# Cross attention of layer 0: spreading the inverse row sums to the channels through DRAM instead of by TensorE transposes

## The chip, the cores and the metric

The kernel runs on one core of a Trainium2 chip. A core has five engines with an instruction stream each: TensorE (PE, matmuls and transposes into PSUM), VectorE (DVE), ScalarE (ACT), GpSimd (POOL) and SyncE (SP, which here only issues DMAs). Each engine works its stream strictly in order and waits on semaphores of the others. Sixteen DMA engines move data between DRAM and the on-chip memory SBUF. The metric is the device time of one execution in microseconds (us), as a median of several runs.

## What is computed

A decoder of two layers on 32 sequences of 128 tokens of 128 channels. Layer 0 is a recurrent mixing block (rwkv), a cross attention over a context, and a mixture of experts; layer 1 is a causal attention, a windowed cross attention and a quantised projection. The change lies in layer 0's cross attention, with 16 heads of 64 channels, whose keys and values are extended by 128 learned memory rows, and in the copies of the rwkv block ahead of it:

```python
q = (queries @ wq_w + wq_b).reshape(B, S, H, DK).transpose(0, 2, 1, 3)
k_ext = jnp.concatenate([keys @ wk_w + wk_b, broadcast(mk)], axis=1)
v_ext = jnp.concatenate([values @ wv_w + wv_b, broadcast(mv)], axis=1)
...
scores = jnp.einsum('bhsd,bhtd->bhst', q, k) / jnp.sqrt(jnp.float32(DK))
attn = jax.nn.softmax(scores, axis=-1)
out = jnp.einsum('bhst,bhtd->bhsd', attn, v)
return out.transpose(0, 2, 1, 3).reshape(B, S, H * DV) @ wo_w + wo_b

# rwkv, per head, for every step t:
state = state * jnp.exp(w_t)[..., None] + k_t[..., None] * v_t[..., None, :]
o_t = jnp.einsum('bhkv,bhv->bhk', state, r_t)
```

## The kernel before

The 32 sequences ("blocks") are worked in ten groups of 2, 2, 2, 4, 4, 4, 4, 4, 4 and 2 blocks. For each group g the kernel records three pieces of work for layer 0: `rwkv(g)`, `xattn0(g)` and `route(g)` (the choice of experts and the scatter of tokens to DRAM). After the ninth group come 22 blocks of expert work, then the rest of the experts and layer 1.

*What sets the order.* Nothing is issued where it is written. The helpers `V`, `A`, `G`, `M` and `S` record an operation for DVE, ACT, POOL, PE or SP with an expected duration, its reads and writes, for a DMA the time to landing, and a wished time `plan.at` (in units of four blocks). `Plan.run` then plays these through against a list of engines, buffers and PSUM banks: at each moment an engine takes the ready operation with the earliest wished time. The table `SHIFTS` adds a correction to the wished time of each kind of operation ("DVE sc# nm#" is the row maximum), one table for each layer. The result is one fixed order on each engine; the expected times only serve to make it. Waits at run time are semaphores that follow from the real tiles. So a change of an operation or of a shift can move every instruction of layer 0.

*`xattn0(g)`.* For each of eight channel chunks c (two heads, 128 channels) PE projects keys, queries and values (L764, L767, L774). Then, for two blocks at a time, `slot` computes scores (L843), DVE takes the negative row maximum (L848), ACT the exponentials with their row sums `xsm` as a by-product (L855), PE transposes the exponentials (L865), and DVE and ACT copy these out of PSUM (L871, L869). `attend` (L796) makes `av`: channels on the partitions, tokens along the free dimension, not yet divided by the row sums.

The row sums stand the other way round, one value for each token (partition), block and head. The division takes these steps: DVE forms the reciprocals `xrs` (L803); POOL widens each to 64 columns (`wide`, L805); PE transposes that, one 128x128 transpose for each block, into the PSUM bank `over` (L810); ACT copies it to SBUF (`overs`, L814); DVE multiplies `av` by it into `xoT` (L816). After eight chunks PE projects `xoT` to the output (L823).

*`rwkv(g)`.* The recurrence runs as eight scans on DVE (L684), one for each j of a head's eight value channels; scan j needs channel j of each head of v and r copied to all eight rows of that head. For groups with `early` set, PE does this with a selecting matmul for each j (L640), and PE also sums the eight products r in PSUM (L694, eight matmuls). For the other groups SP stores v and r to DRAM (`spill_v`, `spill_r`, L646) and loads each j as a broadcast (L650), and POOL adds up the eight products (L690), so that L694 has one matmul. `early` is `g < 3`.

*SP's queue.* All plain DMAs are issued by SP in one order: first loads, then `clear` (L891), which writes 17 MB of zeros to the table `xreg`, then the spills and broadcasts, context loads, and after layer 0's attention the experts' weights (L1107) and token rows (L1114). The weights need the block table, which DVE writes (L1071).

Of the kernel before, what the change touches and what calls it, by code (L numbers as in the profile page):

```python
# [48 lines left out]
for _name, _n in (("wo_b", D), ("bo", D), ("b_proj", D), ("f_b", D), ("d_act", 1)):  # L49
# [22 lines left out]


SHIFTS = [{
    "ACT cen#ps# cen#": 0.09, "ACT cen#ps# sq#": -0.22, "ACT g#ps# gate#": -1.15, "ACT h#ps# wb#": 0.6,
    "ACT k#ps# k#sb#": 1.44, "ACT moe#xnT#p moe#xnT#": -0.38, "ACT over# overs#": 0.06,
    "ACT r#ps# r#sb#": 0.94, "ACT rw#xnp# xp#": -0.02, "ACT sc# nm#": 0.91, "ACT th#": -0.06,
    "ACT tr# eT#": 0.72, "ACT v#ps# v#sb#": 0.7, "ACT w#ps# dec#": -0.97, "ACT xa#xnT#p xa#xnT#": 0.04,
    "ACT xk#ps# xk#": -0.61, "ACT xq#ps# xq#": 0.67, "ACT xv#ps# xv#": 0.59, "DVE": 0.2,
    "DVE av# overs#": -0.05, "DVE bv#ps": 0.83, "DVE bv#row": -1.07, "DVE dec# v#": 1.2, "DVE fw#src": -0.22,  # L80
    "DVE fw#src fwq#amax": 1.29, "DVE fwq#c fwq#t": -1.31, "DVE fwq#ps": 0.06, "DVE fwq#t fwq#c": -0.18,
    "DVE g#ps# gate#": 0.61, "DVE gn#ve# gn#rstd#": -0.7, "DVE hot# hot#": -0.9, "DVE hot# lg#": 0.16,
    "DVE k#sb# v#": 1.38, "DVE k#sb# vc#": -1.41, "DVE la# lb#": 0.54, "DVE lg# m#": 0.29,
    "DVE lg#ps# lg#": 0.03, "DVE m# m#": -1.22, "DVE moe#mv#": 0.17, "DVE moe#mv# moe#ve#": -0.56,
    "DVE moe#y# wb#": -0.35, "DVE pl# hot#": -0.09, "DVE pl#ps# pl#": -0.04, "DVE rw#mv#": 0.97,
    "DVE rw#mv# rw#rstd#": -0.46, "DVE rw#mv# rw#ve#": -0.74, "DVE rw#y#": 0.53, "DVE s# r#": 0.1,
    "DVE s# rc#": -1.02, "DVE sc# nm#": 0.82, "DVE tab#n tab#valid": 0.89, "DVE tab#ps": -0.06,
    "DVE tab#wide": 0.04, "DVE th# moe#xn#": 0.51, "DVE tr# eT#": 0.36, "DVE var#ps# gn#ve#": -0.38,
    "DVE wc#m#": -0.1, "DVE wc#t# wc#": -0.11, "DVE xa#mv#": 0.15, "DVE xa#mv# xa#rstd#": -1.4,
    "DVE xa#mv# xa#ve#": 0.93, "DVE xr# bk#which#": 1.12, "DVE xr#ps# xT#": -0.05, "DVE xsm# xrs#": 0.09,  # L90
    "DVE xv#ps# xv#": 0.17, "DVE xy#": 0.94, "PE both# pl#ps#": -0.47, "PE bv#rep bv#ps": -0.16,
    "PE cen# rw#y#": -0.08, "PE e# tr#": -0.87, "PE eT# eT#": 1.44, "PE eT# xv#": 1.31,
    "PE fwq#t fwq#ps": -0.05, "PE hT# wts#": -0.7, "PE l#mix#g# g#ps#": -0.05, "PE l#mix#k# k#ps#": -0.49,
    "PE l#mix#r# r#ps#": -0.9, "PE l#mix#w# w#ps#": -0.23, "PE moe#xn# moe#xnT#p": -0.52,
    "PE moe#xnT# lg#ps#": 1.22, "PE r# cen#ps#": 0.7, "PE r#sb# rc#": -0.3, "PE rexp# rs#ps#": -0.3,
    "PE rw#xn# rw#xnp#": 0.04, "PE sq# var#ps#": -0.59, "PE tab#n": 1.4, "PE v#sb# vc#": -1.12,
    "PE wc# wc#m#": 0.2, "PE wide# over#": -0.26, "PE wts# xT#": 0.89, "PE xa#ctxT# xk#ps#": -1.44,
    "PE xa#ctxT# xv#ps#": -0.13, "PE xa#xn# xa#xnT#p": -0.73, "PE xa#xnT# xq#ps#": 0.36,
    "PE xp# dd#ps#": -0.95, "PE xq# xk#": 0.14, "PE xr# xr#ps#": 0.23, "POOL": 0.2, "POOL bv#rep": 0.13,
    "POOL cen#": 0.2, "POOL dec#": 0.95, "POOL dx# dd#": 0.3, "POOL fw#src fwq#inv": 0.13,  # L100
    "POOL fwq#scale fwq#t": -0.62, "POOL gate# cen#": 1.44, "POOL gn#rstd# rexp#": 0.61,
    "POOL moe#rstd# moe#off#": 0.17, "POOL moe#ve# moe#rstd#": -0.26, "POOL moe#xn#": 1.24,
    "POOL r# r#": -0.4, "POOL rw#rstd# rw#off#": -1.44, "POOL rw#ve# rw#rstd#": -0.6,
    "POOL xa#rstd# xa#off#": -0.04, "POOL xa#ve# xa#rstd#": 1.22, "POOL xp#": -0.97, "POOL xp# dd#": -0.09,
    "POOL xp# dx#": 0.07, "POOL xrs# wide#": 0.1, "POOL yr# bk#to#": 1.11, "SP": 0.02, "SP r#": 0.45,
    "SP r#sb#": 0.38, "SP v#": 0.57, "SP v#sb#": 0.03, "SP wts# wb#": 1.09, "SP xa#ctxT#": -0.01,
    "SP xr#": 0.64,
}, {
    "ACT av#sa# avssa#": 0.48, "ACT av#wa# avswa#": -1.03, "ACT e#sa#": 3.21, "ACT e#wa#": 7.35,
    "ACT ff#rstd# ff#off#": 8.24, "ACT qkT#ps# qkT#": 3.07, "ACT qkv#ps# qk#": -4.56,  # L110
# [32 lines left out]
class Plan:  # L143
# [10 lines left out]
    SWITCH, KEEP = 0.13, 0.0  # L154
# [28 lines left out]
    def run(self):  # L183
# [10 lines left out]
        free_at = dict.fromkeys(engines, 0.0)  # L194
        room, events, order, t = {}, [], [], 0.0
        turns, modes = {}, dict.fromkeys(engines)
        for o in self.ops:
            banks = [x for x in o[4] if x.pool.space == PSUM]
            for x in o[4]:
                room[x.pool, x.tag] = x.bufs  # L200
                if x.pool.space != PSUM:
                    queue = turns.setdefault((x.pool, x.tag), {})
                    queue.setdefault(x, len(queue))
                    for k in banks if o[0] != "PE" else ():
                        if x not in k.follow:
                            k.follow.append(x)
# [4 lines left out]
        while len(order) < n or events:  # L211
            started = True
            while started:
                started = False
                for e in engines:
                    if free_at[e] > t + 1e-9:
                        continue
                    for k, (_, i) in enumerate(ready[e]):
                        if ready_at[i] > t + 1e-9:
                            continue  # L220
# [8 lines left out]
                        if any(q in turns and max(turns[q][x] for x in xs) >= given[q] + len(xs)  # L229
                               for q, xs in need.items()):  # L230
                            continue
# [12 lines left out]
                        break  # L244
# [33 lines left out]
def decoder_kernel(ctx: ExitStack, tc: tile.TileContext, a: dict, out: bass.AP):  # L278
# [49 lines left out]
    def row(name):  # L328
# [85 lines left out]
    pool.iota(nobody, pattern=[[BLK, NBLK], [P, 2]], base=1 + 2 * NB * T, channel_multiplier=1,  # L414
              allow_small_or_imprecise_dtypes=True)
    spill = {n: dram.tile([P, GB * T], F32, tag=f"spill_{n}", name=f"spill_{n}") for n in "vr"}
    zero = const.tile([P, 4 * ROW], F32, tag="zero", name="zero")
    pool.memset(zero, 0.0)

# [17 lines left out]
    def V(weight, fn, r=(), w=()):  # L437
        plan.op("DVE", weight, fn, r, w)
# [16 lines left out]
    def one(shape, name):  # L455
        return Ring(ps_one, "one", 4, shape, name)
# [293 lines left out]
    def xattn0(g):  # L750
# [8 lines left out]
        for c in range(8):  # L759
# [45 lines left out]
            G(0.74, lambda rs=rs, wide=wide: pool.tensor_copy(wide(), bc(rs(), XD)), [rs], [wide])  # L805
            over = one([P, n, T], f"over{g}_{c}")

            def spread(wide=wide, over=over):
                for b in range(n):
                    pe.transpose(over()[:, b], wide()[:, b].rearrange("p j d -> p (j d)"), ident)  # L810

            M(0.44, spread, [wide], [over])
            overs = wt([P, n, T], "overs", f"overs{g}_{c}", 2)
            A(0.6, lambda over=over, overs=overs: act.copy(overs(), over()), [over], [overs])  # L814
            o = wt([P, n, T], "xoT", f"xoT{g}_{c}", 10)
            V(0.69, lambda o=o, av=av, overs=overs: vec.tensor_mul(o(), av(), overs()), [av, overs], [o])  # L816
# [770 lines left out]
```

## Time and profile before

| | us |
|---|---|
| median of 3 runs | 1507.44 (1505.6 to 1508.62) |
| profiled execution | 1505.67 |
| its span, first to last instruction | 1504.0 |
| PE busy | 1387.6 (92%) |
| DVE busy | 1227.2 (82%) |
| ACT busy | 967.9 (64%) |
| POOL busy | 697.5 (46%) |
| first matmul of the first expert block (L1159) | 835.78 |

The page sums busy time by engine, cuts the span into 40 slices of 37.6 us with one digit of busy share each, and lists groups of instructions: line, engine, operation, tiles (output, arrow, inputs), count, busy time and mean duration. [...] The trace behind the page also holds each DMA packet (size, start, duration) and each increment of a semaphore.

### The profile page before, as it was taken

To read this page: it belongs to the slowest core of one execution; us is meant where nothing else is said; L and a number is where in the kernel's file an instruction comes from. 1 tells how busy PE (TensorE), PEld (TensorE's weight loads), DVE (VectorE), ACT (ScalarE), POOL (GpSimd) and SP (SyncE) were. 2 spreads that over 40 slices of the span, in tenths; PEclk is the share of its full clock that TensorE was granted. 3 is DMA by queue.
4 is the path that set the end of the run, shared out by engine and by line. 5 is a ranking of instruction groups with operands and counts; after the bars stand their busy time and mean duration, and the time that the engine had idled before them with its cause. 6 is when DMAs were issued, how large, how long until landed. Compare 5 with 4: busy or idle time off the path is not lost. (4 is left out here: it accounts for less than half of the span.)

```text
span 1504.0 us, 34761 instructions
## 1 busy us (share of the span) xinstructions
PE 1387.6 (92%) x12957; PEld 1069.1 (71%) x12957; DVE 1227.2 (82%) x2688; ACT 967.9 (64%) x2423; POOL 697.5 (46%) x1010
## 2 busy tenths in 40 slices
PE   6899999999999999999998998987888989999995
PEld 4678777787887878878787887964556656566664
DVE  6899898887878868796656575689999989999996
ACT  2467656676766766565674343446777888888784
POOL 6444554543546235262303466658553552553432
PEclk9999999999999999999999998999999999999997
DMA  9903030301203112020000776823000000000000
GB/s 332 324 24 108 16 123 19 113 30 66 84 1 108 43 63 86 2 79 5 16 2 24 230 210 177 252 81 88 15 12 12 19 12 12 16 8 19 5 9 18
DMA packets 80504, 107.64 MB, mean 72 GB/s; under 512 B 7152, under 2 KB 48624, under 8 KB 80336
## 3 DMA queue, kind: packets, MB, share of 16 engines
q1 hardware_dynamic: 75792, 95.97, 20.3%
q0 software_dynamic: 4544, 9.45, 1.8%
q8 instruction: 103, 1.69, 0.5%
q14 instruction: 65, 0.53, 0.1%
HBM read 73.01 MB, written 32.38 MB: 70 GB/s over the span
## 5 line engine op out<-in xcount | busy, mean ns | idle before, releaser
L855 ACT ACTIVATE e<-sc,nm 128x256 f32<-128x256 f32 x512 | 238.3, 482 | 26.1 <-DVE nm L848 26.0
L848 DVE TENSOR_REDUCE nm<-sc 128x4 f32<-128x1024 f32 x128 | 154.6, 1216 | 26.7 <-PE sc L843 25.8
L865 PE MATMUL tr<-ident,e 128*128 128x128 f32 x1024 | 144.0, 278 | 8.7 <-DVE xoT L816 7.5
L865 PEld LDWEIGHTS tr<-ident,e 128*128 128x128 f32 x1024 | 114.4, 142 | 40.6 <-issue 18.9
L1162 ACT ACTIVATE hT<-h_ps,wb 128x256 f32<-128x256 f32 x156 | 65.6, 470 | 94.2 <-PE h_ps L1159 77.4
L805 POOL COPY wide<-xrs 128x512 f32<-128x512 f32 (+1 forms) x80 | 49.0, 614 | 156.9 <-DVE xrs L803 59.9
L843 PE MATMUL sc<-xk,xq 64*128 64x128 f32 x1024 | 112.2, 296 | 0.0
L690 POOL TENSOR_TENSOR r<-r,r 128x512 f32<-128x512 f32 (+1 forms) x49 | 60.3, 1230 | 111.5 <-DVE r L688 98.7
L869 ACT COPY eT<-tr 128x512 f32<-128x512 f32 x128 | 75.3, 588 | 54.5 <-PE tr L865 50.5
L855 ACT ACTIVATION_READ_ACCUMULATOR e<-sc,nm 128x1 f32 x512 | 109.2, 213 | 0.0
L796 PE MATMUL av<-eT,xv 128*64 128x128 f32 x1024 | 104.1, 282 | 0.4 <-DVE xv L778 0.2
L1183 POOL DMA_INDIRECT ytok<-rw,bk_at x78 | 76.9, 986 | 54.5 <-DVE xT L1134 24.6
L843 PE MATMUL sc<-mkT,xq 64*128 64x128 f32 x1024 | 99.9, 272 | 0.0
L796 PE MATMUL av<-eT,mvx 128*64 128x128 f32 x1024 | 99.9, 274 | 0.0
L843 PEld LDWEIGHTS sc<-xk,xq 64*128 64x128 f32 x1024 | 77.9, 187 | 25.5 <-issue 20.7
L871 DVE COPY eT<-tr 128x512 f32<-128x512 f32 x128 | 86.1, 675 | 7.5 <-PE tr L865 7.0
L684 DVE TENSOR_TENSOR_SCAN s<-dec,v 128x512 f32<-128x512 f32 (+1 forms) x80 | 87.1, 1094 | 1.1
L766 ACT COPY xk<-xk_ps 128x512 f32<-128x512 f32 (+1 forms) x80 | 40.0, 501 | 72.3 <-PE xk_ps L764 67.5
L1340 DVE TENSOR_TENSOR e_sa<-sc_sa,nm_sa 128x1024 f32<-128x1024 f32 x64 | 78.4, 1225 | 6.9 <-ACT ff_xn L506 0.5
L816 DVE TENSOR_TENSOR xoT<-av,overs 128x512 f32<-128x512 f32 (+1 forms) x80 | 46.3, 578 | 45.7 <-PE av L796 40.2
L1340 DVE TENSOR_TENSOR e_wa<-sc_wa,nm_wa 128x1024 f32<-128x1024 f32 x64 | 78.4, 1225 | 6.2 <-DVE nm_wa L1338 0.5
L1338 DVE TENSOR_REDUCE nm_sa<-sc_sa 128x8 f32<-128x1024 f32 x64 | 77.8, 1215 | 6.3 <-PE sc_sa L1325 5.6
(586 smaller groups left out, 3932.0 us busy)
## 6 DMA issues: line engine op xcount, KB each, us to landing
xreg<-zero SPq DMA_DIRECT2D x8, 2112.0 KB
v<-spill_v SPq DMA_DIRECT2D x48, 256.0 KB
r<-spill_r SPq DMA_DIRECT2D x48, 256.0 KB
wk<-in_wexp SPq DMA_DIRECT2D x8, 512.0 KB
wq<-in_wexp SPq DMA_DIRECT2D x8, 512.0 KB
wv<-in_wexp SPq DMA_DIRECT2D x8, 512.0 KB
mkT<-in_wexp SPq DMA_DIRECT2D x8, 512.0 KB
mvx<-in_wexp SPq DMA_DIRECT2D x7, 512.0 KB
```

The lines of the kernel that those rows point to most:

```text
L684: V(1.34, lambda u=u, s=s: vec.tensor_tensor_scan(s(), flat(dec()), u(), 0.0, ALU.mult, ALU.add), [dec, u], [s, ("scan", (g, j))])
L796: pe.matmul(av()[r, b], mvx[:, 2 * c + par] if half else v()[:, b, r], eTs[b // 2]()[:, par, half, b % 2], start=(half == 0), stop=(half = ...
L843: pe.matmul(sc()[:, par, at : at + T], q()[r, b0 + b], mkT[r, c] if half else k()[r, b0 + b], start=True, stop=True)
L848: V(1.22, lambda: vec.tensor_reduce(nm(), sc().rearrange("p j (b k) -> p j b k", k=2 * T), AX.X, ALU.max, negate=True), [sc], [nm])
L855: act.activation(e()[:, par, b], sc()[:, par, b * 2 * T : (b + 1) * 2 * T] .rearrange("p (c k) -> p c k", k=T), AF.Exp, bias=nm()[:, par, ...
L865: pe.transpose(tr()[:, half, b], e()[:, par, b, half], ident)
L869: A(0.6, lambda tr=tr: act.copy(eT()[:, 1], tr()), [tr], [(eT, 1)])
L871: V(0.68, lambda tr=tr: vec.tensor_copy(eT()[:, 0], tr()), [tr], [(eT, 0)])
L1162: A(0.47, lambda f=f: act.activation(hT()[:, f], hid(f), AF.Gelu, bias=wb()[:, f : f + 1]), [(h_ps, f % 2), wb] + ["exp"] * (j < BLK1), [( ...
L1183: d = pool.indirect_dma_start(out=ytok, out_offset=bass.IndirectOffsetOnAxis(ap=at()[:, c : c + 1], axis=0), in_=yr()[:, c], in_offset=None)
L1338: V(1.22, lambda nm=nm, sc=sc: vec.tensor_reduce(nm(), sc(), AX.X, ALU.max, negate=True), [scs[half]], [nm])
L1340: V(1.22, lambda nm=nm, sc=sc, e=e: vec.tensor_add(e(), sc(), bc(nm(), T)), [scs[half], nm], [e])
```

## The change

The reciprocals are laid out as [token, head, block] and no longer go through POOL, PE and PSUM. SP stores them to a small DRAM tile (`line`, four in turn), transposed by the access pattern, and SP loads that tile back so that each of a chunk's two rows of values is copied to the 64 channels of its head, giving `overs`. ACT copies `av` from PSUM to `xoT`, and DVE multiplies `xoT` by `overs` in place, from SBUF. The wished time of the multiplication is n/32 units later than that of the reciprocal (n blocks in the group; a group of four spends n/32 units on each chunk), and the output projection's is later by the same amount than it was; `xoT` has 11 buffers instead of 10. Group 2 takes the way through DRAM for its rwkv copies (`early` becomes `g < 2`). The planner can prefer an operation that keeps PE's present division of its array (rows, columns or whole) over one that changes it, if a shift "KEEP" is set; the table has no such entry, and then the value is zero. The table of shifts for layer 0 is a new one throughout; that of layer 1 is as it was.

```diff
 SHIFTS = [{
-    "ACT cen#ps# cen#": 0.09, "ACT cen#ps# sq#": -0.22, "ACT g#ps# gate#": -1.15, "ACT h#ps# wb#": 0.6,
...
+    "ACT": -0.77, "ACT av# xoT#": -0.13, "ACT cen#ps# sq#": -0.14, "ACT g#ps# gate#": -0.25,
...
+        keep = abs(self.shifts.get("KEEP", 0.0))
...
+                        change = keep and self.ops[i][7] != modes[e]
+                        if change and other is not None and other >= 0:
                             continue
...
+    lines = [dram.tile([2 * GB, T], F32, tag=f"line{i}", name=f"line{i}") for i in range(4)]
...
-        early = g < 3
+        early = g < 2
...
-            rs = sm([P, n, 2], "xrs", f"xrs{g}_{c}")
-            V(0.18, lambda rs=rs, sums=sums: vec.reciprocal(rs(), sums()), [sums], [rs])
-            wide = wt([P, n, 2, XD], "wide", f"wide{g}_{c}", 2)
-            G(0.74, lambda rs=rs, wide=wide: pool.tensor_copy(wide(), bc(rs(), XD)), [rs], [wide])
-            over = one([P, n, T], f"over{g}_{c}")
-
-            def spread(wide=wide, over=over):
-                for b in range(n):
-                    pe.transpose(over()[:, b], wide()[:, b].rearrange("p j d -> p (j d)"), ident)
-
-            M(0.44, spread, [wide], [over])
+            rs = sm([P, 2, n], "xrs", f"xrs{g}_{c}")
+            V(0.18, lambda rs=rs, sums=sums: vec.reciprocal(rs(), sums().rearrange("p b j -> p j b")), [sums], [rs])
+            plan.at, plan.size = begin + n / 32, 1.0
+            line = lines[c % 4]
+            S(0.7, lambda rs=rs, line=line: sync.dma_start(out=line[0 : 2 * n].rearrange("k t -> t k"), in_=rs().rearrange("p j b -> p (j b)")),
+              [rs], [f"line{c % 4}"], 4.0)
             overs = wt([P, n, T], "overs", f"overs{g}_{c}", 2)
-            A(0.6, lambda over=over, overs=overs: act.copy(overs(), over()), [over], [overs])
-            o = wt([P, n, T], "xoT", f"xoT{g}_{c}", 10)
-            V(0.69, lambda o=o, av=av, overs=overs: vec.tensor_mul(o(), av(), overs()), [av, overs], [o])
+            S(0.7, lambda overs=overs, line=line: sync.dma_start(
+                out=overs(), in_=line[0 : 2 * n].rearrange("(j b) t -> j (b t)", j=2).unsqueeze(1).to_broadcast([2, XD, n * T])),
+              [f"line{c % 4}"], [overs], 2.8)
+            plan.size = size
+            o = wt([P, n, T], "xoT", f"xoT{g}_{c}", 11)
+            A(0.6, lambda o=o, av=av: act.copy(o(), av()), [av], [o])
+            plan.at = begin + n / 16
+            V(0.65, lambda o=o, overs=overs: vec.tensor_mul(o(), o(), overs()), [overs], [o])
             outs.append(o)
-        plan.at = start + n / 4
+        plan.at = start + n / 4 + n / 32
```

More of the change, by code (lines that the diff above doesn't have):

```diff
@@ L74 @@
 SHIFTS = [{
-    "ACT cen#ps# cen#": 0.09, "ACT cen#ps# sq#": -0.22, "ACT g#ps# gate#": -1.15, "ACT h#ps# wb#": 0.6,
[L76 to L107, printed above, removed]
+    "ACT": -0.77, "ACT av# xoT#": -0.13, "ACT cen#ps# sq#": -0.14, "ACT g#ps# gate#": -0.25,
@@ new lines @@
+    "ACT h#ps# wb#": 0.31, "ACT k#ps# k#sb#": -0.85, "ACT moe#xnT#p moe#xnT#": 0.04, "ACT r#ps# r#sb#": -1.3,
+    "ACT sc# nm#": 1.36, "ACT tr# eT#": -0.21, "ACT v#ps# v#sb#": -0.55, "ACT xq#ps# xq#": 1.03,
+    "ACT xv#ps# xv#": 1.44, "DVE": -0.37, "DVE bv#ps": 0.72, "DVE bv#row": -0.51, "DVE dec# v#": 0.35,
+    "DVE fwq#t fwq#c": 0.51, "DVE g#ps# gate#": -0.76, "DVE gn#ve# gn#rstd#": -1.36, "DVE hot# hot#": -0.89,
+    "DVE hot# lg#": 0.6, "DVE k#sb# v#": 0.49, "DVE k#sb# vc#": 0.27, "DVE la# lb#": 0.38,
@@ new lines @@
+    "DVE lg# m#": -0.4, "DVE m# m#": -1.44, "DVE moe#mv#": -1.28, "DVE moe#mv# moe#rstd#": -0.04,
+    "DVE moe#mv# moe#ve#": -0.22, "DVE moe#y# wb#": -1.07, "DVE overs# xoT#": 0.15, "DVE pl#ps# pl#": -0.32,
+    "DVE rest# m#": 0.76, "DVE rs#ps# cen#": -1.14, "DVE rw#mv# rw#rstd#": -1.21, "DVE rw#mv# rw#ve#": -0.88,
+    "DVE s# r#": -0.08, "DVE sc# nm#": -0.22, "DVE tab#n tab#valid": 1.36, "DVE tab#wide": 0.29,
+    "DVE th# moe#xn#": 1.16, "DVE tr# eT#": -1.14, "DVE var#ps# gn#ve#": -0.46, "DVE wc#m#": 0.56,
@@ new lines @@
+    "DVE wc#t# wc#": -0.22, "DVE xr#ps# xT#": -0.16, "DVE xsm# xrs#": -0.49, "DVE xv#ps# xv#": -0.85,
+    "PE both# pl#ps#": 0.66, "PE cen# rw#y#": -0.2, "PE e# tr#": -0.1, "PE eT# eT#": 0.45,
+    "PE eT# xv#": 1.31, "PE fwq#t fwq#ps": -0.19, "PE hT# wts#": -1.44, "PE l#mix#g# g#ps#": -1.34,
+    "PE l#mix#k# k#ps#": -0.34, "PE l#mix#r# r#ps#": -0.13, "PE l#mix#v# v#ps#": -1.23,
+    "PE r# cen#ps#": 0.24, "PE r#sb# rc#": 0.68, "PE rexp# rs#ps#": -0.95, "PE rw#xn# rw#xnp#": -0.93,
+    "PE sq# var#ps#": 0.07, "PE tab#n": 0.26, "PE tab#wide tab#ps": 1.41, "PE v#sb# vc#": 0.43,
@@ new lines @@
+    "PE wc#t#": 0.3, "PE wts# xT#": -0.01, "PE xa#ctxT# xk#ps#": -0.19, "PE xa#ctxT# xv#ps#": 0.43,
+    "PE xa#xn# xa#xnT#p": -0.67, "PE xa#xnT# xq#ps#": 0.3, "PE xoT# xoT#": 0.14, "PE xp# dd#ps#": -1.06,
+    "PE xq# xk#": -0.36, "PE xr# xr#ps#": -1.14, "POOL dec#": 1.39, "POOL dx# dd#": -0.74,
+    "POOL fw#src fwq#inv": -0.31, "POOL gate# cen#": 0.63, "POOL moe#rstd# moe#off#": -0.54,
+    "POOL moe#ve# moe#rstd#": 0.31, "POOL moe#xn#": 0.32, "POOL xa#ve# xa#rstd#": 1.07,
+    "POOL xp# dd#": -0.32, "POOL yr# bk#to#": -0.1, "SP bv#row": -0.87, "SP v#sb#": -0.51,
@@ L108 @@
+    "SP wts# wb#": 0.04, "SP xa#ctxT#": -0.08,
 }, {
@@ L151 @@
                 ("DVE", "POOL"): 0.2, ("ACT", "DVE"): 0.07, ("ACT", "POOL"): 0.15, ("POOL", "DVE"): 0.05}
-    SWITCH, KEEP = 0.13, 0.0
+    SWITCH = 0.13
     def __init__(self, shifts):
@@ L217, in run @@
                         continue
-                    for k, (_, i) in enumerate(ready[e]):
+                    other = None
+                    for k, (at, i) in enumerate([*ready[e], (math.inf, None)]):
+                        if other is not None and at > ready[e][other][0] + keep:
+                            k, other = other, -1
+                            i = ready[e][k][1]
+                        if i is None:
+                            break
                         if ready_at[i] > t + 1e-9:
+                            continue
+                        change = keep and self.ops[i][7] != modes[e]
+                        if change and other is not None and other >= 0:
                             continue
@@ L230, in run @@
                                for q, xs in need.items()):
+                            continue
+                        if change and other is None:
+                            other = k
                             continue
```

## The prediction

> **What bounds the kernel now.** I read the page's totals and slices first, then the busy time of each engine by stage, then the groups of the lines that the change touches, and last the queue of SP and the DMA packets.
>
> ```profile
> PE 1387.6 (92%) x12957; PEld 1069.1 (71%) x12957; DVE 1227.2 (82%) x2688; ACT 967.9 (64%) x2423; POOL 697.5 (46%) x1010
> ...
> PE   6899999999999999999998998987888989999995
> ...
> DVE  6899898887878868796656575689999989999996
> ...
> DMA  9903030301203112020000776823000000000000
> ```
>
> The first 22 of 40 slices are the attention part of layer 0. TensorE stands at nine tenths there, VectorE below it, the DMA engines mostly idle. The stages in numbers:
>
> ```profile
> 0.00:70.00 70.00, 51.62 (x244) 39.06 (x245) 52.99 (x148) 22.37 (x57) 36.44 (x82) 0.98 1.00 346
> 70.00:830.00 760.00, 739.80 (x7073) 594.56 (x7074) 610.08 (x1274) 494.90 (x1529) 321.77 (x440) 0.99 0.16 52
> 830.00:1504.00 674.00, 596.17 (x5645) 435.47 (x5641) 564.13 (x1267) 450.67 (x838) 339.29 (x488) 0.97 0.22 65
> ```
>
> Columns: stretch, length, then PE, weight loads, DVE, ACT, POOL, granted clock, DMA share, GB/s. From 70 to 830 us PE is busy 739.8 of 760 us (97%), DVE 80%, ACT 65%, POOL 42%. So PE's work sets this stage, and what is taken off PE there shortens the run; what is taken off ACT or POOL does not. What follows 830 us has the same instructions in the same order in both programs (from expert block 22 on, word for word), so I carry it over unchanged.
>
> **The change part by part.** The division's four steps before:
>
> ```profile
> L810 PE MATMUL over<-ident,wide x256: 272/273/476, 70.5 to 829.1; 128*128 128x128 f32 x128
> L814 ACT COPY overs<-over x80: 352/585/598, 71.7 to 829.5; 128x512 f32<-128x512 f32 x48, 128x256 f32<-128x256 f32 x32
> ...
> L805 POOL COPY wide<-xrs x80: 386/609/1420, 69.2 to 826.2; 128x512 f32<-128x512 f32 x48, 128x256 f32<-128x256 f32 x32
> ...
> L816 DVE TENSOR_TENSOR xoT<-av,overs x80: 390/676/694, 94.9 to 830.8; 128x512 f32<-128x512 f32 x48, 128x256 f32<-128x256 f32 x32
> ```
>
> (1) *PE loses the 256 transposes of L810.* Their own busy time is 42.4 us (0.77 before 100 us, 41.63 after). Matmuls overlap, so that is too much: between 100 and 800 us the groups of PE add up to some 900 us, while PE as a whole was busy 685.5, a factor of 0.76. That gives 32 us. The pitch agrees: eight transposes of tr in a row last 1.09 us, the first 0.27, so 0.117 each, times 256 = 30. I take 32 (30 to 42). PE also stood idle 3.4 us ahead of them between 100 and 800 us: with them gone, −3.
>
> (2) *Third group's copies (two blocks).* It leaves 16 selecting matmuls (L640) and 7 of 8 accumulating ones (L694).
>
> ```profile
> 0.00:100.00 100.00, 27.70 (x96) 18.15 (x96) 0.98 0.71 247
> ...
> 0.00:100.00 100.00, 13.85 (x48) 8.44 (x48) 0.98 0.71 247
> ```
>
> A third of 27.7 is 9.2, 7/8 of a third of 13.85 is 4.0; by 0.76, 10 us. They lie before 100 us, where PE is 74% busy up to 70 us and 93 to 100% after; I count −7 (0 to −13). In exchange: 2 stores and 16 broadcasts of 128 KB on SP, and 7 POOL additions (1.23 us for 512 columns, L690, so about 4.5 us), on an engine 42% busy. These DMAs stand behind the 17 MB of clearing, which SP issues until 54 us; the group's first load in the new order is needed only after the first attention slots, and I count nothing for it. Without that cover the third scan starts up to 5 us late.
>
> (3) *POOL loses 49.0 us of widening copies, ACT swaps one copy from PSUM for another of the same shape (585 ns), DVE multiplies from SBUF* instead of PSUM (676 ns; the all-SBUF product of L688 has a median of 692): 0. One PSUM bank per channel pair is no longer taken, and av's is freed by ACT without waiting for the sums: a small gain, not counted.
>
> (4) *80 stores of single elements.* The store is 128 partitions x 2n values of 4 bytes: 1024 pieces for four blocks, 64 per DMA engine. Issue: the clearing transfers, also 1024 pieces, take SP 1.15 us when nothing holds them. Landing: the spill store (128 pieces of 2 KB) has its last increment 1.68 us after issue in the trace's records. Below: the smallest data packets there, 16 and 32 bytes, last 9 ns, 64 of them 0.6 us, so 2.2 us. Above: no row shows a small write to DRAM. [...] With the 27 ns of a 512-byte packet it is 3.4 us; with the 91 ns of the 2112-byte packets that clear DRAM, the dearest writes there, 7.5. I take 3.0, nearest to the small packets. So each SP pair holds SP for about 1.15 + 3.0 + 0.57 us per slot of 11.6 us.
>
> (5) *80 broadcasts, 256 KB each (128 KB for two blocks).* The nearest row is the broadcast of v and r, same size:
>
> ```profile
> 208.84 0.57 SPq L650 DMA_DIRECT2D v<-spill_v  x1
> 211.30 0.57 SPq L650 DMA_DIRECT2D r<-spill_r  x1
> ...
> 199.00:208.00 9.00, 9.00 (x81) 7.47 (x80) 8.79 (x18) 3.67 (x12) 4.37 (x7) 1.00 0.53 205
> ```
>
> Alone they land 3.2 to 3.8 us after issue. By that row alone the new broadcast costs the same, 3.4 us. But while they run the DMA share is 0.53, not 1, and each load shows eight DMA increments of its semaphore, where the spill store shows sixteen. [...] Their source has 8 copies outermost; the new source is [2 heads, 64 copies, n·128], so only 2 engines work. A 2048-byte packet takes 84 ns: 64 x 84 = 5.4 us, plus the 2.1 that stay of 3.4 after 16 x 84 ns = **7.5 us**; for two blocks 64 x 46 ns = 2.9, so 5.0. [...] By the row alone the sum below would be 7 us shorter.
>
> *Who waits.* The broadcast is waited for by the DVE product, in line with everything on DVE (row maxima, half of eT, the scan). From the order of the changed program: tiles are numbered as the work is issued, 1123 numbers for a group of four, and such a group took 93.1 us (spills of v at 266.44 and 361.46 and so on), about 89 after (1); so 12.6 numbers are 1 us. In groups 3 to 8 the product stands a median of 12.6 us behind its broadcast's issue (shortest 4.7) and 18 behind the reciprocal. Needed: 0.6 + 7.5 = 8.1 behind the issue. 11 of 48 fall short, by 19 us in sum; counted from the reciprocal (12.3 us) it is 9. DVE has some 15% to spare and PE two score banks to live on, so I let half of about 14 reach PE: **+7** (0 to +40). The v and r loads share engines 0 and 1: 8 x 5.4 + 16 x 1.34 = 65 of 89 us, so they are 1 to 5 us later; their products stand near 19 us behind, so 0. SP's element stores also stand ahead of these loads, inside the same slack.
>
> *Tail.* In the last group only two overs buffers exist, and two products (the fifth and sixth channel pairs) stand ahead of the write of the block table, which the expert weights on SP need; the weights stand behind the last broadcast. From the product of the fourth pair: fifth 5.6 us, sixth 8.5, seventh 11.8, eighth 14.6, output projection and first expert matmul near 19, 20 from the last reciprocal. Before it was 13.8 us (822.03 to 835.78). PE has 7.3 us of work in it instead of 5.6, so **+5** (0 to +12).
>
> (6) *A new order of all of layer 0.* PE's idle time outside the tail is 14 us, so there is nothing to win and something to lose: +3 (−5 to +15). The keep rule in the planner is idle: no shift of that name is set, so it is zero.
>
> Sum: −32 − 3 − 7 + 7 + 5 + 3 = **−27**. The profiled execution took 1505.67 us (span 1504.0), so 1478.7; against the median of 1507.44, **1480 us** (−1.8%).
>
> **The rivals.**
> - *Full gain (0.13).* The broadcasts hide and the order is as tight as before: −45 from the first three terms and +3 for the tail, about 1465. For it: median slack 12.6 us. Against: 11 short places.
> - *Gain eaten (0.14).* Stalls reach PE in full and the tail is late: −42 + 19 + 12 + 8, about 1503 (1497 to 1514). Measured as no change from 1504.4 to 1510.5, since this kernel can tell about 0.2%.
> - *Slower (0.18): the element store.* SP waits for it in order, so each extra microsecond goes to the broadcast and then to DVE. With a reciprocal-to-product need of 16 us the shortfall is 47 us, with 20 us 138. It decides when the store lands some 8 us after issue rather than 3, where shortfall that reaches PE passes the gain of 42. At 10 us (need 19.3) the shortfall is some 120; a stall also delays what comes after, so I let 60% count: 1507 − 42 + 70 = 1535. For it: no row prices 4-byte writes, and 7.5 us is within the bounds. Against: small packets of 9 ns.
> - *The order is not realised*, PE having been busy for other reasons: excluded by 97% busy at a granted clock of 0.99; only its gaps could grow.
>
> **How the numbers follow.** Likeliest case 0.55: 1480, its own range 1468 to 1494. Range for all: low 1460 (leaves out 0.06), high 1522 (leaves out about 0.13). Faster: 0.55 + 0.13 + 0.04 of the third case = 0.72; same: 0.05; slower: 0.05 + 0.18 = 0.23.
>
> **What would show it.** Right: no over group; PE near 97% busy from 70 to about 800 us; expert blocks starting near 810 instead of 836; broadcasts of overs on two increments landing near 7.5 us; DVE idle before xoT a few tens of us at most, released by DMA. Wrong: DVE idle ahead of xoT over 80 us, SP waiting on the element store for more than 5 us each, PE below 93%; or overs landing after 3.4 us, which would refute the two engines.

## The result: 23% slower

The changed kernel takes 1860.14 us (median of 4 runs, 1855.71 to 1862.52); the kernel before took 1508.03 us (1505.6 to 1510.33) on the same chip. The ratio is 1.2332, 95% interval 1.2301 to 1.2363. The prediction, 1480 us in 1460 to 1522, was wrong in sign and in size.

The page of the changed kernel (totals; slices of 46.4 us; DMA packets):

```profile
PE 1437.8 (77%) x12655; PEld 1092.1 (59%) x12655; DVE 1210.9 (65%) x2688; ACT 969.4 (52%) x2423; POOL 653.5 (35%) x937
...
PE   6855665578696696693887968798978899999986
...
DVE  6744454556684574573566525374789998999996
...
PEclk9977787789798798796898989798999999999998
...
DMA packets 160184, 127.02 MB, mean 68 GB/s; under 512 B 74288, under 2 KB 122160, under 8 KB 160016
```

PE has some 300 matmuls fewer, as intended, and is busy 50 us longer. Packets under 512 bytes were 7152 and are 74288: the element stores are nearly all of the difference. The same stages as before, with the border moved to the first expert block (first matmul at 1186.8 us, before 835.8); the columns are those of the prediction's stage table:

```profile
0.00:70.00 70.00, 52.52 (x256) 38.75 (x257) 48.93 (x145) 21.89 (x56) 35.17 (x81) 0.95 1.00 337
70.00:1185.00 1115.00, 791.01 (x6800) 620.47 (x6798) 598.70 (x1283) 496.70 (x1529) 278.94 (x368) 0.84 0.30 54
1185.00:1857.50 672.50, 594.26 (x5601) 432.85 (x5601) 563.22 (x1263) 450.79 (x838) 339.38 (x488) 0.97 0.22 64
```

What follows the attention part takes 672.5 us, before 674.0 (cut a few us before the first expert matmul in both): nothing was lost there. All of the 353 us of span lie between 70 and 1185 us, where PE was 97% busy and now is 71%. DVE does the same work there as before (598.7 and 610.1 us), over 1115 us instead of 760. Who waits, from the groups and then the waits (engine, line, what it waited for; us in total, times, longest):

```profile
L821 DVE TENSOR_TENSOR xoT<-xoT,overs 128x512 f32<-128x512 f32 (+1 forms) x80 | 48.2, 603 | 314.8 <-DMA overs<-line 310.3
```
```profile
DVE xoT L821 <- DMA overs<-line: 310.3, 44, 25.4
ACT e L860 <- DVE nm L853: 283.4, 49, 22.5
...
DVE v L688 <- DMA v<-spill_v: 60.0, 9, 16.4
...
DVE r L693 <- DMA r<-spill_r: 28.1, 7, 11.6
```

DVE stands still 310 us ahead of the division, 44 times, for the broadcast of the inverse sums, and another 88 us for the v and r loads of the recurrence. ACT's 283 us are the same stalls one step on: DVE works in order, so the row maxima that the next exponentials need stand behind the waiting product. In the kernel before, the division waits for PE and not for a transfer, no wait for a v or r load is listed, and ACT waits a tenth as long:

```profile
DVE xoT L816 <- PE av L796: 40.2, 31, 5.2
...
ACT e L855 <- DVE nm L848: 26.0, 27, 3.0
```

SP's own queue shows where the broadcast is late:

```profile
SPq L814 <- DMA line<-xrs: 491.7, 49, 20.4
...
SPq L811 <- DMA overs<-line: 110.3, 17, 10.7
```

L814 is the broadcast's issue: SP waits 10 us a time, 49 times, for the element store of L811; the next stores (L811) in turn wait for earlier broadcasts. From the trace's semaphore records (last increment after the end of the issue) the store lands after a median of 10.67 us (8.37 at least, 20.35 at most). The broadcast lands after 10.45 (for four blocks 6.75 at least), on three increments: one some 0.42 us after the issue, as each v load has too, then two. A v load, with 8 copies outermost in its source, has eight after the first, a store from 128 partitions sixteen; so I read the two as two DMA engines, one for each of the source's two heads. The loads of v went from a median of 3.81 to 7.39 us, those of r from 6.68 to 10.67.

### The profile page after: what moved, and what is told of

Its sections match the earlier page's. It is cut to its first block, busy times and chain, and to the rows that moved or that the text cites. A ratio compares the mean times of both kernels' runs of the same rounds, so it can differ in the third digit from the quotient of the medians.

```text
span 1857.5 us, 34239 instructions
## 1 busy us (share of the span) xinstructions
PE 1437.8 (77%) x12655; PEld 1092.1 (59%) x12655; DVE 1210.9 (65%) x2688; ACT 969.4 (52%) x2423; POOL 653.5 (35%) x937
## 2 busy tenths in 40 slices
DMA packets 160184, 127.02 MB, mean 68 GB/s; under 512 B 74288, under 2 KB 122160, under 8 KB 160016
## 5 line engine op out<-in xcount | busy, mean ns | idle before, releaser
L821 DVE TENSOR_TENSOR xoT<-xoT,overs 128x512 f32<-128x512 f32 (+1 forms) x80 | 48.2, 603 | 314.8 <-DMA overs<-line 310.3
L695 POOL TENSOR_TENSOR r<-r,r 128x512 f32<-128x512 f32 (+1 forms) x56 | 67.8, 1211 | 442.3 <-DVE r L693 349.9
L870 PE MATMUL tr<-ident,e 128*128 128x128 f32 x1024 | 158.4, 295 | 81.2 <-DVE eT L876 27.8
L848 PE MATMUL sc<-xk,xq 64*128 64x128 f32 x1024 | 120.6, 313 | 2.9 <-issue 2.1
L779 PEld LDWEIGHTS xv_ps<-wv,xa_ctxT 128*128 128x128 f32 x512 | 76.3, 214 | 76.2 <-DVE eT L876 52.6
L779 PE MATMUL xv_ps<-wv,xa_ctxT 128*128 128x128 f32 x512 | 80.8, 302 | 49.9 <-DVE eT L876 48.1
L801 PEld LDWEIGHTS av<-eT,xv 128*64 128x64 f32 x1024 | 65.4, 147 | 73.6 <-DVE eT L876 27.9
L772 PE MATMUL xq_ps<-xa_xnT,wq 128*128 128x512 f32 (+1 forms) x160 | 78.6, 583 | 36.5 <-DVE eT L876 31.6
L769 PE MATMUL xk_ps<-xa_ctxT,wk 128*128 128x512 f32 (+1 forms) x160 | 79.3, 585 | 22.4 <-DVE eT L876 19.1
L828 PE MATMUL xy<-wo,xoT 128*128 128x128 f32 x512 | 72.4, 304 | 23.7 <-DVE xoT L821 22.7
```

The source lines that it names most:

```text
L769: M(0.87, lambda c=c, ks=ks: pe.matmul(ks(), wk[:, c * P : (c + 1) * P], cT(), start=True, stop=True), [cT, "wk"], [ks])
L772: M(0.87, lambda c=c, qs=qs: pe.matmul(qs(), wq[:, c * P : (c + 1) * P], xnT(), start=True, stop=True), [xnT, "wq"], [qs])
L779: pe.matmul(vs()[:, b], cT()[:, b], wv[:, c * P : (c + 1) * P], start=True, stop=True)
L801: pe.matmul(av()[r, b], mvx[:, 2 * c + par] if half else v()[:, b, r], eTs[b // 2]()[:, par, half, b % 2], start=(half == 0), stop=(half = ...
L848: pe.matmul(sc()[:, par, at : at + T], q()[r, b0 + b], mkT[r, c] if half else k()[r, b0 + b], start=True, stop=True)
L870: pe.transpose(tr()[:, half, b], e()[:, par, b, half], ident)
```

## The experiments

Every run is compared with the kernel before on its own chip: 1515.96 us for the contiguous store, the split broadcast, both together and the table alone; 1519.15 for the stores that nobody reads, the told planner, the third group alone and the first of the two kernels of transfers; 1514.51 (median of 15) for the other four. Where a kernel ran once there is no interval; the 15 runs lie within 1511.3 to 1519.0, so a difference of a few us means nothing.

**The store or the broadcast.** First the changed kernel with the store's pieces made contiguous: each partition's values go as one piece of 16 or 32 bytes. The broadcast then reads them in the wrong order, so this kernel divides by other tokens' sums.

```diff
-sync.dma_start(out=line[0 : 2 * n].rearrange("k t -> t k"), in_=rs()...)
+sync.dma_start(out=line[0 : 2 * n].rearrange("k t -> (k t)").rearrange("(t k) -> t k", t=P), in_=rs()...)
```

> The changed kernel with the store of the inverse sums made contiguous: each of the 128 tokens writes its 2n values as one piece of 32 bytes (16 for two blocks) instead of 2n pieces of 4 bytes to 2n places. The layout in DRAM is then the wrong one, so the division is by values of other tokens; every instruction, its order and its bytes stay. If the landing of the element store (9.7 us from issue alone, 10.7 in the median) is what costs: it lands in about 1.7 us, the need from reciprocal to product falls from about 18 us to 10, the DMA waits ahead of the product fall from 310 us to under 30, and the run to 1480 to 1500. If it is the broadcast on two DMA engines (64 x 84 ns = 5.4 us each, 43 of 89 us for a group): the waits stay over 100 us and the run over 1600. If the new order is bad: over 1700.

Measured: 1546.41 us, 2.0% above the kernel before instead of 23%. That is the first theory in kind, but 46 us above its range. The store lands after a median of 2.55 us, the v loads after 5.91. The wait for the broadcast shrinks from 310 us not to under 30 but to

```profile
DVE xoT L821 <- DMA overs<-line: 62.3, 19, 7.0
```

Then the other half alone, with the strided store kept: the broadcast as two transfers, one for each head, with 64 copies outermost, which was to bring all 16 engines in.

```diff
-sync.dma_start(out=overs(), in_=line[0 : 2 * n].rearrange("(j b) t -> j (b t)", j=2).unsqueeze(1).to_broadcast([2, XD, n * T]))
+[sync.dma_start(out=overs()[j * XD : (j + 1) * XD], in_=line[j * n : (j + 1) * n].rearrange("b t -> (b t)")
+     .unsqueeze(0).to_broadcast([XD, n * T])) for j in range(2)]
```

> The changed kernel with the broadcast issued as two DMAs, one for each head, whose outermost dimension is the 64 copies on both sides, so that 16 DMA engines share each; the order on every engine is as in the changed kernel, SP has 80 issues more. The broadcast should land about 3 us after issue instead of 7.3 to 10. If the landing of the element store costs: only 4 to 5 of some 18 us are won, waits ahead of the product stay at 100 to 200 us, the run near 1650 to 1750. If the occupation of DMA engines 0 and 1 is the limit (8 x (5.4 + 7.5) + 21.5 = 125 us for a group, measured 130): it falls to about 87 us and the run to near 1500. If the order is bad: over 1700.

Measured: 1775.52 us, still 17.1% above. The range for a costly store was 1650 to 1750, so the time lies above it, where a bad order could be at work too. The broadcasts land in 4.30 us instead of 10.45, the store in 9.78, and the waits stay:

```profile
DVE xoT L821 <- DMA overs<-line: 202.0, 32, 19.5
...
DVE v L688 <- DMA v<-spill_v: 47.6, 8, 17.2
```

Both together (other tokens' sums again):

> Both edits at once (contiguous store, so the division again takes other tokens' values; broadcast on 16 engines). Need from reciprocal to product about 6 us, under the shortest distance in the order (9.8). If the transfers are the whole cause: no DMA wait ahead of the product worth naming, 1465 to 1485, the gain that was forecast without its stall term. If the new order is bad by itself: over 1530.

Measured: 1495.93 us, 1.3% below the kernel before. Its waits, and the stage from 70 us to its first expert block:

```profile
DVE xoT L821 <- DMA overs<-line: 12.0, 5, 3.8
```
```profile
70.00:818.00 748.00, 711.08 (x6807) 567.39 (x6806) 611.29 (x1293) 496.64 (x1529) 290.41 (x370) 0.99 0.26 80
```

PE is back at 95% of the stage and at the clock of 0.99. The order of the instructions is the changed kernel's; only the two transfers differ. So it is not the order that costs, and the two transfers are the whole loss: mending the store alone takes the time from 23.3% above to 2.0%, the broadcast alone to 17.1%. The miss against the expectation (1465 to 1485) is discussed with the order below.

**Landing late for its reader, or holding up others.** In the kernel before I added the 80 strided stores, which nobody reads; the order of all other instructions stays.

```diff
-V(0.18, lambda rs=rs, sums=sums: vec.reciprocal(rs(), sums()), [sums], [rs])
+V(0.18, lambda rs=rs, sums=sums, line=lines[c % 4]: [vec.reciprocal(rs(), sums()),
+     sync.dma_start(out=line[0 : 2 * n].rearrange("k t -> t k"), in_=rs().rearrange("p b j -> p (b j)"))], [sums], [rs])
```

> The kernel before, with PE's division, and the 80 element stores of the inverse sums besides, which nobody reads; the order on all other engines is that of before. If the stores cost only the one who waits for their landing: within 5 us of before. If they also hold up what stands behind them on the DMA engines or on SP: the v and r loads land 5 to 10 us later, and the run is 10 to 60 us longer.

Measured: 1681.08 us, +162. The v loads land after 14.72 us (3.81 before), the r loads after 15.31 (6.68). The second theory holds, and its 10 to 60 us were far too few. But SP now also waits in order for the reciprocals, which could be the cause as well:

```profile
DVE v L683 <- DMA v<-spill_v: 76.9, 10, 14.5
```
```profile
SPq L803 <- DVE xrs L803: 386.5, 53, 24.8
```

So the same stores once more with contiguous pieces, which leaves SP's waits in place:

> The kernel before with 80 stores that nobody reads, as in the run with the strided stores alone (+162 us), but each partition's values now go as one piece of 16 or 32 bytes. What SyncE waits for in its queue stays the same. If the 4-byte pieces hold up the transfers behind them, most of the 162 us goes: within 25 us of the kernel before on the same chip, and the v and r loads land again near 3.8 and 6.7 us. If SyncE's wait for the reciprocals, in order, was the cost, the time stays over 100 us above the kernel before.

Measured: 1518.72 us, +4. SP waits as much as ever:

```profile
SPq L803 <- DVE xrs L803: 412.7, 63, 18.8
```

and the v and r loads land after 3.76 and 4.97 us. So SP's wait costs next to nothing, and 80 strided stores that nobody reads cost some 158 us (162 less 4, each on its own chip). DVE's waits for v and r loads are 92 us of it; the list of waits has one wait for a store itself, 6.5 us, until its buffer was free again. The rest was not attributed wait by wait.

**The transfers by themselves.** Two kernels hold transfers only, each store waited for before the next; nothing of the decoder is computed and their output is zeros.

> Only transfers, nothing of the decoder (the output is zeros): stores of one 128-partition tile to DRAM one at a time, each followed by a small load that waits for it, three rounds. Element stores of 8, 4, 2 and 1 values of 4 bytes per partition (64, 32, 16, 8 pieces for each DMA engine); 8 values in pieces of 8, 16 and 32 bytes; the broadcast of 256 KB from one DMA with two rows outermost, and as two DMAs with 64 copies outermost; and one such DMA directly behind an element store. If each 4-byte write to DRAM is dear: landing falls in line with the number of pieces, from about 9.7 us with 64 toward 1.5 to 2.3 with 8, some 0.13 us a piece, and pieces of 8, 16 and 32 bytes land at about 5.5, 3.5 and 1.6. If the strided layout has a fixed price whatever the number: all element stores land near 9 us. Broadcast: 7.3 us from two rows, 2.5 to 3 in two DMAs. Behind an element store a broadcast lands late, near the store's own landing, if a DMA's increment has to wait for the writes ahead of it on its engine; at its own 2 to 3 us if not.

In SP's queue each store, or group of transfers, is followed by a small read of what was written; that read starts when the store has landed. From the second round (start, duration, operation): a store of 128 pieces of 4 bytes, one of 128 pieces of 32 bytes, and last two halves of a broadcast around a strided store:

```profile
148.59 0.35 SPq L313 DMA_DIRECT2D four<-src  x1
156.17 0.21 SPq L307 DMA_DIRECT2D probe<-four  x1
...
170.06 0.35 SPq L317 DMA_DIRECT2D wide<-src  x1
171.54 0.21 SPq L307 DMA_DIRECT2D probe<-wide  x1
...
196.07 0.45 SPq L331 DMA_DIRECT2D o<-two  x1
196.57 0.59 SPq L329 DMA_DIRECT2D behind<-src  x1
197.21 0.57 SPq L331 DMA_DIRECT2D o<-two  x1
207.62 0.23 SPq L307 DMA_DIRECT2D probe<-behind  x1
```

Both of the first two stores have 128 pieces; the one of 4 bytes takes 7.2 us, the one of 32 bytes 1.1. All three rounds, by the semaphore records:

| transfer | landing after issue, us |
|---|---|
| 4-byte pieces, 1024 / 512 / 256 / 128 of them (medians) | 10.99 / 8.52 / 8.01 / 7.17 |
| the same 4 KB in pieces of 8 / 16 / 32 bytes (medians) | 3.91 / 1.18 / 1.07 |
| broadcast of 256 KB, two heads outermost | 6.57 to 6.99, three increments |
| broadcast as two transfers, 64 copies outermost | 2.26 to 2.41 each |
| such a transfer directly behind a strided store | 8.03 to 10.64 (the store itself: 8.47 to 11.09) |

A transfer behind the strided store lands only when the store does, as the expectation had it for increments that wait for the writes ahead: 8.03 to 10.64 us, where the store takes 8.47 to 11.09. The packet records agree: the packets of that transfer have all ended some 2.0 us after its issue, as they do without a store ahead; only its increments come late. In one of the three rounds even the half issued just ahead of the store was late (7.5 us; 2.5 and 2.3 in the others). Neither the number of pieces (an eighth of them still takes two thirds of the time) nor the bytes explain the store. So the second kernel moved the pieces apart in DRAM:

> Transfers alone, nothing of the decoder is computed (its output is zeros). Stores of 1024 pieces of 4 bytes, each piece 1, 2, 4, 8, 16 and 128 words from its neighbour in DRAM; of 128 pieces of 4 bytes 8 and 128 words apart; and of 1024 and 128 pieces of 512 bytes. If neighbours inside one stretch of DRAM wait for each other, the landing falls as the distance grows, from about 11 us at 1 word to under 4 us at 8 words or at 16, and the 128 pieces fall from 7 us to under 3. If every write of 4 bytes is slow by itself, all of the 1024 stay at 8 to 13 us whatever the distance and the 128 stay at about 7. If the count of pieces is what costs, 1024 pieces of 512 bytes land no sooner than 1024 of 4.

In the second round, 1024 pieces of 4 bytes whose neighbours are 4, 8 and 16 bytes on; then 128 pieces 32 bytes apart; last the store that was meant to have 1024 pieces of 512 bytes:

```profile
71.39 0.37 SPq L314 DMA_DIRECT2D gap<-src  x1
82.64 0.24 SPq L308 DMA_DIRECT2D probe<-gap  x1
84.28 0.37 SPq L314 DMA_DIRECT2D gap<-src  x1
88.75 0.49 SPq L308 DMA_DIRECT2D probe<-gap  x1
91.69 0.36 SPq L314 DMA_DIRECT2D gap<-src  x1
94.63 0.49 SPq L308 DMA_DIRECT2D probe<-gap  x1
...
113.08 0.33 SPq L318 DMA_DIRECT2D one<-src  x1
114.83 0.49 SPq L308 DMA_DIRECT2D probe<-one  x1
...
121.44 0.32 SPq L322 DMA_DIRECT2D long<-wide  x1
124.12 0.49 SPq L308 DMA_DIRECT2D probe<-long  x1
```

| from one 4-byte piece to the next in DRAM | landing, three rounds, us |
|---|---|
| 4 bytes | 11.93 (behind the store of the output), 10.82, 8.34 |
| 8 bytes | 3.98, 4.03, 4.50 |
| 16 bytes | 2.29, 2.51, 2.77 |
| 32, 64, 512 bytes | 1.98 to 2.85 |
| 128 pieces: 32 bytes | 1.72, 1.35, 1.08 |
| 128 pieces: 512 bytes | 1.06 to 1.07 |
| for comparison 128 pieces of 4096 bytes | 2.28 to 2.29 |

The comparison is not the one that was meant: the trace has 128 packets of 4096 bytes for it; a partition's eight pieces lie side by side on both sides. It isn't needed. Landing falls with the distance, as the theory that neighbours wait for each other had it, and already 16 bytes are enough: 2.29 to 2.77 us, where 32 to 512 bytes give 1.98 to 2.85. The theories that each small write is slow by itself, or that the count of pieces is what costs, fall: 1024 pieces of 4 bytes, 16 bytes apart, land within 2.3 to 2.8 us.

**Is it the planner, which was told too short a landing?** The changed kernel with 9.7 and 7.3 us for the store and the broadcast in place of 4.0 and 2.8:

```diff
-[rs], [f"line{c % 4}"], 4.0)
+[rs], [f"line{c % 4}"], 9.7)
...
-[f"line{c % 4}"], [overs], 2.8)
+[f"line{c % 4}"], [overs], 7.3)
```

> The changed kernel with the planner told the landing times that were measured (9.7 us for the store, 7.3 for the broadcast, instead of 4.0 and 2.8); the transfers and the rest as they are. If only latency is at fault and a better order can hide it: 1500 to 1600. If the DMA engines 0 and 1 are held (about 125 us for a group of four) or the two buffers for the values are too few: still over 1700.

Measured: 1802.31 us, 18.6% above the kernel before on its chip, and DVE still waits 245.7 us for the broadcast. An order made with longer landing times recovers less than five of the 23 points. The times told are still short of the 10.67 and 10.45 of the full kernel, so how much the best order could hide stays open.

**The order.** The kernel before with the changed kernel's table of shifts for layer 0:

> The kernel before with nothing changed but the table of shifts of layer 0, taken from the changed kernel: TensorE division and three early groups as before. If the order is not the cause: within 1500 to 1530. If the new table is bad by itself: over 1550.

Measured: 1534.86 us, +19, just above the range. And the kernel before with `early = g < 2` alone:

> The kernel before with the third group's copies through DRAM alone (early for two groups); the planner makes its own order from the old table. As forecast: 7 us less (0 to 13) if the order is as good; 10 to 30 us more if the old table does not fit.

Measured: 1534.05 us, +15, where the instructions taken off PE let me expect −7, had the table still fitted. Both fit a table that is good only for the list of operations that it was made for; in the second DVE also waits 12 us for v and r loads, all in the first 150 us, where none is listed before, so the copies themselves may be the cost as well. Neither says what the new table costs in the new list.

**A version with the store mended.** TensorE turns the inverse sums into rows, VectorE copies these to SBUF, the store writes 2n rows of 512 bytes, and the broadcast goes as two transfers.

```diff
+rp = one([2 * n, T], f"rp{g}_{c}")
+M(0.12, lambda rs=rs, rp=rp: pe.transpose(rp(), rs().rearrange("p j b -> p (j b)"), ident), [rs], [rp])
+rt = sm([2 * n, T], "xrt", f"xrt{g}_{c}")
+V(0.2, lambda rt=rt, rp=rp: vec.tensor_copy(rt(), rp()), [rp], [rt])
+S(0.7, lambda rt=rt, line=line: sync.dma_start(out=line[0 : 2 * n], in_=rt()), [rt], [f"line{c % 4}"], 2.0)
```

> The changed kernel with the strided store mended: TensorE turns the inverse sums (128 x 2n) into rows (2n x 128), VectorE copies them to SBUF, the store writes 2n rows of 512 bytes, and the broadcast goes as two transfers, one for each head. All is computed. The contiguous store with the 16-engine broadcast took 1495.9 us (20 below the kernel before on its chip); 80 transposes at 0.12 us and 80 small copies at some 0.15 us add 10 to 20 us of work and one more hand-over to each chunk. Theory (transfers were the loss): 1485 to 1515 us, ratio 0.98 to 1.00. Rival (the new order and the longer path from the sums to the division were a loss by themselves): over 1520 us.

Measured: 1514.45 us, ratio 1.0001 (0.9984 to 1.0019): no difference. The store lands in 0.94 us, the broadcasts in 2.29, and little is left of the division's wait:

```profile
DVE xoT L824 <- DMA overs<-line: 4.6, 2, 2.5
```

So the bound is PE again, at 94% of the stage from 70 to 860 us. What is new in it:

```profile
L812 PE MATMUL rp<-ident,xrs x80: 269/273/273, 72.2 to 813.0; 128*8 128x128 f32 x48, 128*4 128x128 f32 x32
L814 DVE COPY xrt<-rp x80: 229/269/280, 73.4 to 813.7; 8x128 f32<-8x128 f32 x48, 4x128 f32<-4x128 f32 x32
```

80 single transposes last 273 ns each and 80 copies of 8 or 4 rows 269 ns, together 21.5 us of DVE's work, where I had counted 0.15 each. PE is busy 13 us longer than in the run with both transfers mended, DVE 9. That is of the size of the 20 us between the two (1.3% of the time); that it is the cause is argued, not shown.

The same with the kernel before's table and its three copied groups:

> The same mended spread, with the kernel before's table of shifts and its three copied groups. The new table in the old kernel cost 19 us by itself; if that is a property of the table and not of its fit, this is 10 to 20 us faster than the mended spread with the new table: 1470 to 1500 us. If a table fits only the list of operations that it was made for, it is within 10 us of that one or slower.

Measured: 1526.97 us, ratio 1.0082 (1.0054 to 1.0109). The old table, which beats the new one in the old kernel by 19 us, loses to it here by 12.5, with the third group's copies back on PE. That fits a table tied to its list; the two differences were not run apart. No kernel tried computes everything and beats the kernel before.

## Why the prediction was wrong

**(1) and (2), PE loses work: right in kind, too high.** With both transfers mended PE is busy 1358.3 us against 1387.6, so 29 less; the two steps had 32 and 10 us of busy time, 42 in sum. The profile before is from another chip, so this is good to some us.

**(3) The swaps at nothing: right.** ACT's copy has a median of 586 ns (585 before), DVE's product 681 (676).

**(4) The element store: the step that failed.** It had "I take 3.0, nearest to the small packets", with 7.5 as the upper bound. It lands after 10.67 us, and the bound was no bound: I priced the pieces one after another by packet durations, and the packets are indeed short (a median of 7 ns). What takes the time shows in no packet row. The issue was cheaper than I had it, 0.37 us instead of 1.15. The trace before held no small neighbouring writes, so no row could bound it. I said as much ("no row shows a small write to DRAM") and still gave the short end most of the chance.

With each partition's values in one piece the run took 1546 us, where the changed kernel's ratio makes 1869 on that chip (1.2332 x 1515.96). That alone does not tell the number and the size of the pieces from their places. But stores of pieces of 4 to 32 bytes that start 16 bytes or more apart land within 1.1 to 2.9 us, so being small is not what made this store dear.

A second step failed with it: under "Who waits" the store mattered only to its own reader. It had "SP's element stores also stand ahead of these loads, inside the same slack", put the v and r loads "1 to 5 us later", and counted 0 for them. The stores that nobody reads cost 158 us, with contiguous ones as control; the whole change cost 352.

**(5) The broadcast: its own time nearly right, its place wrong.** The 7.5 us were an estimate that rests on two engines, carried over from the v and r loads with their 8 copies and eight increments. No row of the trace before shows such a broadcast; the changed kernel's has two increments after the first, and by itself it took 6.6 to 7.0 us. In the kernel it takes 10.45: there it stands behind the element stores of other chunks and beside the v and r loads, and in the transfers by themselves half a broadcast behind an element store took 8.0 to 10.6 us instead of 2.3. With 0.4 us from the reciprocal to the store's issue, 10.7, 0.5 and 10.4 a chunk needs 22 us from reciprocal to product. The slack that I read from the order was the right instrument. By the same estimate some 30 of the 48 chunks of groups 3 to 8 fall short of 22 us, by 165 to 200 us in sum with 12.6 to 13.5 numbers to a microsecond, where the prediction's 12.3 us gave 9. Over all 80 chunks the trace has 310 us of waits. The tail grew too: from the last scores to the first expert matmul 42.8 us, before 21.5; with both transfers mended 28.6, so +7 for the order itself, where I had +5.

**(6) The new order at +3: not settled.** Without the stalls (+7) the prediction's sum is −34; both transfers mended gave −20. The table alone costs +19 in a list that it was not made for, and this cannot be carried over.

**The rival that came closest** was "the element store", at 0.18: right mechanism, right threshold (about 8 us), wrong price. It had 1535 us at a landing of 10 us, because I let only 60% of the shortfall count against PE, left out the broadcast's own delay by the stores, and gave the v and r loads nothing. Measured: +352, not +28. DVE stood 310 + 88 us, and the changed kernel's span is 363 us above that of the run with both transfers mended, which has the same order: nearly as much as DVE stood. That PE has only two score banks to work ahead on would explain why so little was hidden; no run varied that, and PE's lower clock (0.84 in this stage against 0.99) is in the 363 us too.

The signs of being wrong that were written down all came: DVE idle 310 us ahead of the product (over 80), SP waiting 10 us for each element store (over 5), PE at 71% (below 93). So did one of the signs of being right, the broadcast on two increments.

## What to carry to other kernels

A column of values that goes to DRAM element by element should be turned into rows on chip first (here the rows landed in 0.94 us, the elements in 10.67), or kept on chip: pieces that lie side by side and are written separately are what costs here, not small pieces as such (1024 pieces of 4 bytes: 8.3 to 11.9 us side by side, 2.3 to 2.8 us 16 bytes apart). Price a transfer by what stands behind it on the DMA engines as well as by its reader; the 80 stores that nobody read cost 158 us here. Where no row of the trace shows an operation, a bound from packet durations is no upper bound, and the chance of the bad case should say so; one run of that transfer alone would have shown some 11 us, past the 8 us at which the prediction's own sum turns against the change.

## What the runs showed of the hardware

- *Separate writes of neighbouring bytes.* 1024 writes of 4 bytes each land in 8.3 to 11.9 us side by side, in 4.0 to 4.5 us 8 bytes apart and in 2.3 to 2.8 us 16 bytes apart. 8-byte pieces side by side took 3.9 us, 16-byte pieces 1.2. Writes that share 16 bytes and wait for each other would explain the order of these figures; the wait itself, and whether the DRAM or the DMA engines make it, no run shows. In the changed kernel 910 of one store's 1024 packets start within one microsecond, and its increments come 7.1 to 9.7 us after the issue: the time lies behind the start of the writes.
- *Such a store holds back the landing of what follows it.* Transfers behind it land with it, at 8.0 to 10.6 us instead of 2.3, though their packets have ended some 2.0 us after the issue with or without it.
- *The granted clock falls with the stalls.* In the traces' clock records PE has either the full clock or half of it, the half for 3.4 us or a multiple. From 70 us to the first expert block the kernel before has 2 stretches at half clock, 10 us in sum, and no gap between two matmuls as long as the shortest such stretch, 3.4 us. The changed kernel has 35, 358 us in sum, and 30 longer gaps; the run with the broadcast mended 30 and 22, the one with both transfers mended 3 and 1. The mean clock of the stage was 0.84, 0.87 with the broadcast mended, 0.97 with the store made contiguous (70 to 830 us) and 0.99 in the two runs with both transfers mended. Gaps and stretches rise together in these four runs; that a gap brings on a stretch is my reading, and no run varied it alone. PE's busy time in this stage was 791.0 us, against 711.1 for the same instructions with both transfers mended. How much of the 352 us the clock adds was not measured apart.
